# A vision transformer tower on one core: tokenizer and both attentions in an order written by hand, with a causal sum over tokens

## The chip, the core and the metric

The kernel runs on one core of a Trainium2 chip. The metric is the device time of one execution in microseconds (us). TensorE (PE in the profile) multiplies matrices and turns tiles, VectorE (DVE), ScalarE (ACT) and GpSimd (POOL) do the elementwise work, and SyncE (SP) issues most transfers. [...]

## What is computed

Thirty-two images of 256 x 256 x 3 are cut into 256 patches of 768 values and projected to 256 features. Two layers follow, each with an attention and a feed-forward part on layer-normalised features. Everything is float32.

```python
h = patches @ W.T + b                                   # tokenizer
# layer 0, gating attention:  xn = rms-normalised layernorm(h)
uv = silu(xn @ W_uv + b_uv); u, v, base = split(uv)
q, k = base * gamma[0] + beta[0], base * gamma[1] + beta[1]
h = h + (u * (relu(q @ k.T / sqrt(128)) ** 2 @ v)) @ W_o + b_o
# layer 0, feed-forward on the 127 best-ranked of 256 tokens (x = layernorm(h))
w = x @ wr + br;  y = (gelu(x[sel] @ w1 + b1) @ w2 + b2) * w[sel]
h = h + x + scatter(y)
# layer 1, phase attention (x = layernorm(h))
key, query = (tanh(gelu(x @ W1 + b1) @ W2 + b2) * freq * pi for both)
retrieved = causal sum over tokens of cos(query - key) * (x @ Wv + bv), / sqrt(positions * 64)
h = h + x + (layernorm(retrieved) * ln_w + ln_b) @ Wo + bo
# layer 1, attention experts: 4 heads x 4 experts, causal softmax, gates;
# the residual of head n is the projection of image n by head n, for all images
resid = sx[arange(4), arange(4)]
```

## The kernel before

All features H stay in on-chip memory, as one tile of 128 partitions x 2 x 256 per image. `bank()` (ppool) gives one of eight accumulator banks of 512 columns. `mm` (L114) is every matrix product, in float32, and appears in the profile as two passes of PE per product. `transposed` (L187) turns features with eight PE passes per pair of images; `copy_split` evicts the first half on ACT (L192) and the second on DVE (L194). `normed` (L173) makes layer-normalised features on DVE, `stats` (L122, L123) the mean and variance of a chunk, and `pow_rstd` (L147, L148) the inverse root on POOL.

There are five stages:

- **Tokenizer** (`unit_a`): one image per step, 24 passes of 256 columns, patches loaded by SP six images ahead.
- **Gating attention** (`unit_b`): one pair of images per unit, in five sections that `phase` staggers. The first normalises (L173), turns, and makes base, q and k (L394, L396). The second makes scores, gates (`uT`) and values (`bv`). The third makes the gated product (`gT`, L439), the output product, H (L452) and its statistics. The fourth is `norm_c` with the token weights (L341), the fifth `ranks`: `rank_c` turns the weights of an image into a bank (L349), DVE counts how many tokens are ahead (L354, L356), and POOL scatters the tokens to DRAM by rank (L365).
- **Feed-forward** (`step_c`): quads of images through w1 and w2; DRAM transfers gather the results. From step 8 on each step also takes one section of `prepare`, which folds the weights for layer 1.
- **Phase attention** (`turn`, `hidden`, `phases`, `values_d`, `match`, `memory`, `turn_back`, `output`): pairs of images, three steps apart. `memory` multiplies the causal match of keys and queries (`dat`) with the values (`dv`); the result is turned back and multiplied with wo1 in `output`. At step 21 `residuals` normalises, turns and projects images 0 to 3.
- **Experts** (`prep`, `scores`, `weights`, `values`, `post`): images six steps apart, in an order written out by hand.

Who sets the order differs by stage. Inside `tc.manual_schedule(engines=...)` each named engine gets its instructions in the order of the program text; elsewhere a planner orders them by its own costs. Before the change the tokenizer is written by hand for PE, ACT and SP only, the feed-forward and experts' loops for all five queues, and both attentions are left to the planner. The phase attention's program text is steered by

```python
ORDER = ((1, turn), (7, output), (4, match), (2, hidden), (5, memory), (3, phases), (6, turn_back),
         (3, values_d), (0, norm))
```

Of the kernel before, what the change touches and what calls it, by code (L numbers as in the profile page):

```python
# [31 lines left out]
F32 = mybir.dt.float32  # L33
# [6 lines left out]
P = 128  # L40
# [38 lines left out]
def vit_tower(tc, a, out):  # L79
# [116 lines left out]
    def one_step(active):  # L196
        return [g for g in active if next(g, g) is not g]

    def phase(unit, images, steps):

        active = []
        for b in range(0, B, images):
            active = one_step([unit(b)] + active)
        for _ in range(steps - 1):
            active = one_step(active)
        return active


# [35 lines left out]
    patches = a["patches"].rearrange("(k p) t -> p k t", p=P)  # L247
    with (
        tc.tile_pool(name="a_w", bufs=1) as pw,
        tc.tile_pool(name="a_x", bufs=6) as pp,  # L250
        tc.manual_schedule(engines={ENG.PE, ENG.Activation, ENG.SP}),
# [35 lines left out]
        loaded = []  # L287
        st_b = new_stats("b")

        def unit_a(b):  # L290
# [20 lines left out]
            if b == 4:  # L311
                loaded.extend(layer_0_weights())
            if b % 2:
                factors_b(b - 1)
            yield

        def factors_b(b):


            st, rs, i = at(st_b, b)  # L320
            q = slice(i * NC, (i + 2) * NC)
            var = st.rearrange("p i c s -> p (i c) s")[:, q, 1]
            low = spool.tile([P, 2 * NC], F32, name="low")
            pow_rstd(low, var)
            nc.gpsimd.tensor_scalar(rs[:, q], var, 1e-36, 1.0, ALU.max, ALU.mult)
            nc.gpsimd.tensor_tensor(rs[:, q], rs[:, q], minus_half[:, 0 : 2 * NC], ALU.pow)
            nc.vector.scalar_tensor_tensor(rs[:, q], low, 1e5, rs[:, q], ALU.mult, ALU.min)
            nc.vector.tensor_scalar(rs[:, q], rs[:, q], col("attn_g"), None, ALU.mult)

        phase(unit_a, 1, 2)  # L330
        wuv, row_b, wo, row_c, before, w1 = loaded

    def norm_c(b):
        x = px.tile([P, NC, D], F32, name="cx", bufs=6)
# [34 lines left out]
    with (  # L369
# [4 lines left out]
        scale = 1.0 / math.sqrt(128.0)  # L374

        def unit_b(b0):
            xs = []
            for j in range(2):
                x = p4.tile([P, NC, D], F32, name="bx")
                normed(x, b0 + j, st_b)  # L380
                xs.append(x)
                nc.gpsimd.tensor_tensor(
                    H[b0 + j], H[b0 + j], over(row_b("b_o"), [P, NC, D], 1), ALU.add
                )
            xT = p2.tile([P, 2, 2 * N], F32, name="bxT")
            transposed(xT, xs, copy_split)

            base = p2.tile([P, 2 * N], F32, name="base")
            p = bank()
            for k in range(2):  # L390
                mm(p, wuv[:, k, 1024:1152], xT[:, k, :], k == 0, k == 1)
            nc.scalar.activation(base, p, AF.Silu, bias=col("b_base"))
            q = p2.tile([P, 2 * N], F32, name="bq")
            nc.vector.tensor_scalar(q, base, col("gamma", 0), col("beta", 0), ALU.mult, ALU.add)  # L394
            kk = p2.tile([P, 2 * N], F32, name="bk")
            nc.vector.tensor_scalar(kk, base, col("gamma", 1), col("beta", 1), ALU.mult, ALU.add)  # L396

            yield
            attn = []
            for j in range(2):  # L400
                p = bank()
                for m in range(NC):
                    mm(p[:, m * N : (m + 1) * N], kk[:, j * N + m * P : j * N + (m + 1) * P], q[:, j * N : (j + 1) * N])
# [4 lines left out]
                attn.append(t)  # L408

            uT = p2.tile([P, 4, 2 * N], F32, name="uT")  # L410
            for hc in range(4):
                p = bank()
                for k in range(2):
                    mm(p, wuv[:, k, hc * P : (hc + 1) * P], xT[:, k, :], k == 0, k == 1)
                nc.scalar.activation(uT[:, hc, :], p, AF.Silu, bias=col("b_u", hc))
            vs = []
            for tb in range(2 * NC):
                p = bank()
                for k in range(2):
                    mm(p, xT[:, k, tb * P : (tb + 1) * P], wuv[:, k, 512:1024], k == 0, k == 1)  # L420
# [3 lines left out]
                vs.append(v)  # L424

            yield
            gTs = []
            for j in range(2):
                gT = p2.tile([P, 4, N], F32, name="gT")
                for half in range(2):  # L430
                    p = bank()
                    for h in range(2):
                        hc = 2 * half + h
                        for m in range(NC):
                            mm(
                                p[:, h * N : (h + 1) * N], vs[j * NC + m][:, hc * P : (hc + 1) * P],
                                attn[j][:, m, :], m == 0, m == NC - 1,
# [3 lines left out]
                        uT[:, 2 * half : 2 * half + 2, j * N : (j + 1) * N], ALU.mult,  # L441
                    )
                gTs.append(gT)
            if b0 == B - 2:
                turn_c(0, quads[0], 0)
            for j in range(2):
                b, gT = b0 + j, gTs[j]
# [8 lines left out]

            pow_rstd_of(st_c, b0, 2)

            yield
            normed_c[b0] = [norm_c(b0 + j) for j in range(2)]  # L460

            yield
            ranks(b0)
            if b0 in (2, 6):
                first_ranks(b0 - 2, quads[b0 // 4], 0)
# [9 lines left out]
        phase(unit_b, 2, 3)  # L475
# [26 lines left out]
    wv, wo1 = load(pwd, "wv1", nc.sync), load(pwd, "wo1", nc.sync)  # L502
# [3 lines left out]
    add_row = pwd.tile([P, D], F32, name="add_row")  # L506
    row_e = load_rows(pwe, "rows_e", ROWS_E, N_ROWS_E, nc.sync)
# [46 lines left out]
    def prepare():  # L554


        for w, g in ((wv, 2), (row_d("bv").unsqueeze(1), 1)):
# [3 lines left out]
            nc.vector.tensor_tensor(w, w, over(m, [P, g, D], 2), ALU.subtract)  # L561
        nc.gpsimd.memset(ones_row, 0.0)
# [10 lines left out]
        for k in range(2):  # L573
            mm(p[:, 0:D], col("ln_b", k).to_broadcast([P, P]), wo1[:, k, :], k == 0, k == 1)
        pa, pv = bank(), bank()
# [7 lines left out]
        nc.vector.tensor_tensor(add_row, p[:, 0:D], row_d("bo"), ALU.add)  # L583
# [49 lines left out]
        yield  # L633
        for k in range(2):
            nc.vector.tensor_scalar(wo1[:, k, :], wo1[:, k, :], col("ln_w", k), None, ALU.mult)
# [23 lines left out]
    def residuals(pool):  # L659
        for n in range(NH):  # L660
            xT = features(pool, normed_e(pool, n))
            p = bank()
            for c in range(NC):
                for k in range(2):
                    mm(
                        p[:, c * HD : (c + 1) * HD], xT[:, k, c * P : (c + 1) * P], hl[:, k, n * HD : (n + 1) * HD],
                        k == 0, k == 1,
                    )
            nc.vector.tensor_tensor(
                res[:, :, n, :], p[:, 0 : NC * HD].rearrange("p (c d) -> p c d", c=NC),  # L670
                over(row_e("hl_b")[:, n * HD : (n + 1) * HD], [P, NC, HD], 1), ALU.add,
            )
        centred(res8, res8, NC * NH)

# [4 lines left out]
    def norm_d(b0, s, pool, name, bufs):  # L679
        s.xs = []  # L680
        for j in range(2):
            x = pool.tile([P, NC, D], F32, name=name, bufs=bufs)
            normed(x, b0 + j, st_d)
            s.xs.append(x)
            h = H[b0 + j]
            nc.gpsimd.tensor_tensor(h, h, x, ALU.add)
            nc.gpsimd.tensor_tensor(h, h, over(add_row, [P, NC, D], 1), ALU.add)

    with region_c:
# [20 lines left out]
        def fetch(b0, s, half):  # L710
            s.y = s.y if half else []
            for b in range(b0 + 2 * half, b0 + 2 * half + 2):
                y = px.tile([P, NC, D], F32, name="cx", bufs=6)
# [889 lines left out]
```

## Time and profile before

| what | before |
|---|---|
| median of 3 runs (lowest, highest) | 2049.75 us (2048.95, 2054.02) |
| the profiled execution | 2053.58 us, span 2051.8 us |
| PE busy | 1973.4 us (96%) |
| DVE / ACT / POOL busy | 1334.2 / 832.5 / 731.1 us |
| mean granted PE clock | 0.977 |
| tokenizer, first to last product | 9 to 173 us of the span |
| gating attention | 173 to 712 us |
| feed-forward | 712 to 956 us |
| phase attention | 956 to 1333 us |
| experts and the end | 1333 to 2052 us |

The span is the time on the profiler's clock from the first to the last instruction; the execution's own time is 1.8 us longer. A share is busy time over the span. The stage borders are read from the timeline at the last product of a stage. The chain of waits that ended last lies to 90% on PE.

### The profile page before, as it was taken

The page shows a single profiled execution, that of the slowest core. Times are in us where ns is not written, and L with a number is a line of the kernel's source. Part 1 is how long each engine was busy: PE and PEld are TensorE (multiplying, and loading weights), DVE is VectorE, ACT ScalarE, POOL GpSimd, SP SyncE. Part 2 cuts the span into 40 slices and gives each one's busy share as a digit, 9 for nine tenths or more (in the row PEclk, how much of TensorE's full clock was granted, in tenths as well). Part 3 has the DMA queues.
Part 4 walks back from the last instruction along what each step waited for, and adds up shares of the span by engine and source line. Part 5 has one row for each costly group of instructions (what it writes and reads, how often), then busy time and mean ns, then how long its engine had stood idle before and what let it go on. Part 6 is the DMA issues. An engine that isn't in the chain of part 4 may idle for free.

```text
span 2051.8 us, 38271 instructions
## 1 busy us (share of the span) xinstructions
PE 1973.4 (96%) x15412; PEld 1431.7 (70%) x15412; DVE 1334.2 (65%) x3591; ACT 832.5 (41%) x1569; POOL 731.1 (36%) x691
## 2 busy tenths in 40 slices
PE   9998999999999899999999999999999999999983
PEld 8885676666667657666667677667777777777762
DVE  2335557667675634435655566547898989998986
ACT  0001322222221121222443444367777777777762
POOL 1224224334341443336432333103444444444443
PEclk9999999999999999999998999989999999999996
DMA  9540000000000222221000000001121212121212
GB/s 296 151 135 1 0 1 31 18 24 16 16 18 29 87 81 72 60 70 57 1 0 1 1 1 1 1 17 38 39 63 43 64 43 63 44 62 45 64 48 53
DMA packets 69687, 95.12 MB, mean 46 GB/s; under 512 B 8576, under 2 KB 50944, under 8 KB 69120
## 3 DMA queue, kind: packets, MB, share of 16 engines
q1 hardware_dynamic: 62784, 75.04, 13.1%
q0 software_dynamic: 6144, 16.79, 2.7%
q8 instruction: 123, 2.02, 0.4%
q10 hardware_dynamic: 576, 0.79, 0.1%
q14 instruction: 60, 0.49, 0.1%
HBM read 46.45 MB, written 20.97 MB: 33 GB/s over the span
## 4 chain that ended last, share of the span: by engine, by line
PE 90%; DVE 5%; DMA 1%; ACT 1%; issue 1%; POOL 1%; SPq 0%; DVEq 0%; ACTq 0%; POOLq 0%
PE bank L114 85%; PE bank L646 2%; PE bank L187 2%; PE bank L1148 1%; DMA both<-hx 1%; PE bank L349 1%; DVE bank L994 0%; ACT bxT L192 0%; DVE fout L1157 0%; PE bank L240 0%; DMA patch<-in_patches_dram 0%; DMA cx<-results,rank_of 0%; DVE six L122 0%; DVE two L1079 0%; DVE fout L1153 0%
## 5 line engine op out<-in xcount | busy, mean ns | idle before, releaser
L996 ACT ACTIVATE et<-bank 128x512 f32<-128x512 f32 x384 | 202.4, 598 | 59.0 <-DVE bank L994 58.3
L114 PEld LDWEIGHTS bank<-ev,et 128*64 128x64 f32 x6144 | 198.0, 137 | 33.8 <-ACT et L996 21.3
L994 DVE TENSOR_TENSOR bank<-bank,w_tri 128x256 f32<-128x256 f32 (+1 forms) x384 | 173.6, 514 | 69.6 <-PE bank L114 67.6
L114 PE MATMUL bank<-ev,et 128*64 128x74 f32 (+1 forms) x6144 | 210.9, 226 | 0.0
L1074 POOL TENSOR_TENSOR eo<-eo,gate 128x1024 f32<-128x1024 f32 x64 | 121.9, 1925 | 226.5 <-DVE gate L1071 207.9
L114 PE MATMUL bank<-g,sx 64*128 64x512 f32 (+1 forms) x512 | 192.7, 506 | 0.7 <-ACT g L954 0.7
L114 PE MATMUL bank<-g,sw 64*128 64x512 f32 (+1 forms) x512 | 191.8, 506 | 0.0
L114 PE MATMUL bank<-tokW,patch 128*128 128x256 f32 x768 | 166.7, 380 | 2.3 <-DMA patch<-in_patches_dram 2.3
L114 PEld LDWEIGHTS bank<-tokW,patch 128*128 128x128 f32 x768 | 146.1, 190 | 23.0 <-issue 2.7
L114 PE MATMUL bank<-bxT,w_wuv 128*128 128x512 f32 x320 | 149.2, 605 | 5.5 <-ACT bxT L192 3.9
L192 ACT COPY bxT<-bank 128x512 f32<-128x512 f32 x16 | 9.4, 586 | 342.6 <-PE bank L187 342.6
L1026 POOL TENSOR_TENSOR hv<-hv,minus_half 128x8 f32<-128x8 f32 x64 | 119.5, 1867 | 5.3
L1012 ACT COPY eo<-bank 128x286 f32<-128x286 f32 x256 | 97.2, 421 | 58.3 <-PE bank L114 51.8
L114 PE MATMUL bank<-xsel,w_w 128*128 128x512 f32 x256 | 113.3, 600 | 0.0
L114 PE MATMUL bank<-attn,bv 128*128 128x256 f32 x512 | 113.3, 379 | 0.0
L114 PE MATMUL bank<-w_wo,gT 128*128 128x256 f32 x512 | 113.1, 379 | 0.0
L114 PE MATMUL bank<-w_w,hT 128*128 128x256 f32 x512 | 113.1, 379 | 0.0
L114 PE MATMUL bank<-w_wuv,bxT 128*128 128x512 f32 x256 | 112.5, 592 | 0.0
L114 PEld LDWEIGHTS bank<-attn,bv 128*128 128x128 f32 x512 | 97.1, 190 | 19.5 <-issue 6.9
L114 PEld LDWEIGHTS bank<-w_w,hT 128*128 128x128 f32 x512 | 96.7, 190 | 15.8 <-issue 3.3
L114 PEld LDWEIGHTS bank<-w_wo,gT 128*128 128x128 f32 x512 | 97.2, 190 | 13.2
L114 PEld LDWEIGHTS bank<-bxT,w_wuv 128*128 128x128 f32 x320 | 59.8, 192 | 66.3 <-issue 53.0
(245 smaller groups left out, 3980.2 us busy)
## 6 DMA issues: line engine op xcount, KB each, us to landing
patch<-in_patches_dram SPq DMA_DIRECT2D x31, 768.0 KB, 4.7
sw<-sx SPq DMA_DIRECT2D x64, 128.0 KB, 2.4
both<-fxT SPq DMA_DIRECT2D x64, 128.0 KB, 2.5
both<-hx SPq DMA_DIRECT2D x64, 128.0 KB, 2.3
out_dram<-fout SPq DMA_DIRECT2D x32, 256.0 KB, 2.5
cs<-ranked SPq DMA_DIRECT2D x32, 128.0 KB, 3.0
results<-cy SPq DMA_DIRECT2D x32, 128.0 KB, 1.7
w_w<-in_w_dram SPq DMA_DIRECT2D x2, 1024.0 KB, 10.2
```

The costliest lines, as they stand in the source:

```text
L114: nc.tensor.matmul(o, lhsT, rhs, start=first, stop=last)
L187: nc.tensor.transpose(p[:, o : o + P], x[:, c, k * P : (k + 1) * P], ident)
L192: nc.scalar.copy(o, i)
L349: nc.tensor.transpose(pw[:, c * P : (c + 1) * P], w[:, c : c + 1].to_broadcast([P, P]), ident)
L646: nc.tensor.transpose(p[:, o : o + P], x[:, c, k * P : (k + 1) * P], ident)
L994: nc.vector.tensor_tensor(own, own, over(tri, [P, n_e, P], 1), ALU.add)
L996: nc.scalar.activation(t, p, AF.Exp)
L1012: nc.scalar.copy(im.o[:, c * NH + n, 0:OC], p[:, 0:OC])
L1026: nc.gpsimd.tensor_tensor(v, v, minus_half, ALU.pow)
L1074: nc.gpsimd.tensor_tensor(im.mix[k], im.mix[k], over(im.gate[:, :, 2 * k : 2 * k + 2], [P, NC * NH, 2, HD], 3), ALU.mult)
L1148: nc.tensor.transpose(im.po[:, o : o + P], im.fT[:, k, c * P : (c + 1) * P], ident)
```

## The change

All five queues are put under the written order from the start of the tokenizer to the end of the phase attention (`by_hand`). The generator-based `unit_b` becomes separate functions (`norm_b`, `turn_b`, `base_b`, `queries_b`, `scores_b`, `gates_b`, `values_b`, `gated_b`, `output_b`) in one loop. The first two pairs are normalised after images 26 and 28 of the tokenizer, and the first pair is turned and multiplied to base, q and k before the last image. In each later step the ranks stand between base and queries, and the next pair is normalised at the end.

```diff
+    by_hand = ExitStack()
+    by_hand.enter_context(tc.manual_schedule(engines={ENG.PE, ENG.DVE, ENG.Activation, ENG.Pool, ENG.SP}))
...
+    def norm_b(b0, s):
+        s.xs = []
+        for j in range(2):
+            x = px.tile([P, NC, D], F32, name="cx", bufs=8)
+            normed(x, b0 + j, st_b)
+            s.xs.append(x)
+            h = H[b0 + j]
+            nc.gpsimd.tensor_tensor(h, h, over(row_b("b_o"), [P, NC, D], 1), ALU.add)
...
+        for b in range(B):
+            if b == B - 1:
+                half = [p0.tile([P, 4, D], F32, name="cs", bufs=2).rearrange("p j d -> p (j d)") for _ in range(2)]
+                turn_b(0, pairs_b[0], p0, "xsel")
+                base_b(0, pairs_b[0], half[0][:, 0 : 2 * N])
+                queries_b(0, pairs_b[0], half[0][:, 2 * N :], half[1][:, 0 : 2 * N])
+            unit_a(b)
+            if b == 4:
+                wuv, row_b, wo, row_c, before, w1 = layer_0_weights()
+            if b % 2:
+                powers = powers_b(b - 1)
+            elif b:
+                factors_b(*powers)
+            if b in (B - 6, B - 4):
+                u = (b - B + 6) // 2
+                norm_b(2 * u, pairs_b[u])
...
+        for t in range(B // 2 + 2):
+            def pair(u):
+                return (2 * u, pairs_b[u]) if 0 <= u < B // 2 else None
+
+            new, old, older = pair(t) if t else None, pair(t - 1), pair(t - 2)
+            if new:
+                turn_b(*new, p2, "bxT")
+                base_b(*new, p2.tile([P, 2 * N], F32, name="base"))
+            if t >= 4:
+                ranks(2 * (t - 4))
+                if t in (5, 7):
+                    first_ranks(2 * t - 10, quads[t // 2 - 2], 0)
+            if new:
+                queries_b(*new, p2.tile([P, 2 * N], F32, name="bq"), p2.tile([P, 2 * N], F32, name="bk"))
+            if old:
+                scores_b(*old)
+                gates_b(*old)
+                values_b(*old)
+            if t == 1:
+                factors_b(*powers)
+            if t >= 3:
+                normed_c[2 * (t - 3)] = [norm_c(2 * (t - 3) + j) for j in range(2)]
+            if older:
+                gated_b(*older)
+                if t == B // 2 + 1:
+                    turn_c(0, quads[0], 0)
+                output_b(*older)
+            if 2 <= t + 1 < B // 2:
+                norm_b(*pair(t + 1))
```

In the phase attention the causal sum runs over the tokens' features themselves, and Wv and Wo are applied afterwards in one product of 512 columns: `wvo` holds wv beside wv times wo1, `memory` multiplies the features xs with `dat`, and `output` multiplies the sum with wvo. The first 256 columns give the statistics of the retrieved values, the other 256 are added to H by `add_output` one step later. `values_d` and `turn_back` are gone. The biases go into the features and weights: `norm_d` makes features plus one, and `prepare` subtracts what the one adds (`bias_d`, `add_row`, and bv spread over wv).

```diff
+        q = bank()
+        for k in range(2):
+            mm(q[:, 0:D], ones_d, wv[:, k, :], k == 0, k == 1)
+        for i, w in enumerate((wk1, wq1)):
+            for m in range(2):
+                o = D + 2 * i + m
+                for k in range(2):
+                    mm(q[:, o : o + 1], w[:, k, m * P : (m + 1) * P], ones_d[:, 0:1], k == 0, k == 1)
...
+                nc.tensor.transpose(p[:, o : o + P], wv[:, k, m * P : (m + 1) * P], ident)
...
+                mm(p[:, k * D : (k + 1) * D], wvT[:, m, k * P : (k + 1) * P], wo1[:, m, :], m == 0, m == 1)
+        nc.vector.tensor_copy(wvo[:, :, D:], p.rearrange("p (k d) -> p k d", k=2))
...
+                t, x, p = s.t[j], s.xs[j], bank()
+                for k in range(2):
+                    o, d = k * N, slice(k * P, (k + 1) * P)
+                    mm(p[:, o : o + N], x[:, 0, d], t[:, 0:N], True, False)
+                    mm(p[:, o + P : o + N], x[:, 1, d], t[:, N : N + P], False, True)
+                m = p8.tile([P, 2, N], F32, name="dm", bufs=4)
+                nc.scalar.copy(m.rearrange("p k n -> p (k n)"), p)
...
+        def output(b0, s):
+            st_m = spool.tile([P, 2 * NC, 2], F32, name="d_st")
+            s.po = []
+            for q in range(2 * NC):
+                m, c, p = s.m[q // NC], q % NC, bank()
+                for k in range(2):
+                    mm(p, m[:, k, c * P : (c + 1) * P], wvo[:, k, :], k == 0, k == 1)
+                six = spool.tile([P, 6], F32, name="six")
+                nc.vector.bn_stats(six, p[:, 0:D])
+                nc.vector.bn_aggr(st_m[:, q, :], six)
+                s.po.append(p)
...
+            do(1, turn)
+            do(7, add_output)
+            if t != 4:
+                do(4, match)
+            do(7, stats_e)
+            do(1, residual_d)
+            do(2, hidden, 0)
+            if t == 5:
+                match(0, pairs[0])
+            do(2, hidden, 1)
+            do(5, memory)
+            do(3, phases)
+            if t:
+                do(0, norm_d, p8, "dx", 4)
+            do(6, output)
+            if 3 <= t <= 5:
+                step_c(END_C + t - 3)
```

`residuals` is gone as well: in the experts' stage `prep` projects the turned features of each of the images 0 to 3, which it has anyway, with head b's weights and stores them in `res`.

```diff
+                if b < NH:
+                    p = bank()
+                    for c in range(NC):
+                        for k in range(2):
+                            mm(
+                                p[:, c * HD : (c + 1) * HD], im.xT[:, k, c * P : (c + 1) * P],
+                                hl[:, k, b * HD : (b + 1) * HD], k == 0, k == 1,
+                            )
...
+                if b == NH - 1:
+                    centred(res8, res8, NC * NH)
```

## The prediction

> **What bounds the kernel now.** I read the page's engine totals and slices first, then the busy time by stretch, cut at the stage borders, then the timeline at those borders and inside one period of each stage. TensorE (PE) is busy for 1973.4 of 2051.8 us, and the chain of waits puts 90% on it, so a cost or a gain counts only where it makes PE work longer or stand still. The stretches (columns: length, then PE, PEld, DVE, ACT, POOL busy and instruction count, granted clock, DMA share, GB/s):
>
> ```profile
> 173.00:205.60 32.60, 26.77 (x72) 12.98 (x72) 20.30 (x35) 10.14 (x16) 15.66 (x14) 0.84 0.00 1
> 205.60:667.00 461.40, 457.88 (x1670) 303.46 (x1671) 294.12 (x721) 108.50 (x170) 158.58 (x148) 1.00 0.05 17
> 667.00:721.00 54.00, 45.12 (x183) 32.64 (x183) 37.96 (x126) 7.77 (x12) 22.63 (x25) 0.94 0.28 89
> 978.00:1101.00 123.00, 122.97 (x596) 84.63 (x598) 74.00 (x187) 51.87 (x72) 44.38 (x46) 0.99 0.00 1
> 1101.00:1121.00 20.00, 16.09 (x88) 13.89 (x85) 8.34 (x21) 6.47 (x10) 1.20 (x2) 0.74 0.00 1
> ```
>
> The reader should see that the gating attention (205.6 to 667) and the phase attention (978 to 1101) leave PE almost no gap, while the three borders (tokenizer to gating, gating to feed-forward, the residuals at 1101) do. So the written order has little to win inside the first attention and can only lose there; its gains lie at the borders and in PE work that vanishes.
>
> One period of the gating attention, from the timeline (start, length, engine, line):
>
> ```profile
> 513.83 2.00 DVE L173 TENSOR_SCALAR bx<-h,st_b,rs_b 128x256 f32<-128x256 f32 x3
> ...
> 525.97 7.07 PE L114 MATMUL bank<-w_wo,gT 128*128 128x256 f32 x32
> ...
> 533.07 0.69 DVE L452 TENSOR_TENSOR h<-h,bank 128x512 f32<-128x512 f32 x1 [1.76 <-PE bank L114]
> 533.09 1.04 PE L187 MATMUL bank<-ident,bx 128*128 128x128 f32 x8
> ```
>
> The normalised features bx (L173) were made 19 us before PE turns them (L187). PE starts the turn at 533.09 right behind the output product, while DVE only begins to add that product (L452). The period is 33.06 us (T at 500.04 to 533.09). PE's own work in it: 16 passes of 512 columns each for gates and values at 0.43 us (13.8), 32 of 256 each for gated and output at 0.2155 (13.8), scores 8 x 0.2155 (1.7), base 4 x 0.43 (1.7), 12 turns at 0.12 (1.45): 32.5. Only 0.55 us waits.
>
> How two image ranks follow each other when the order is written, in the feed-forward stage:
>
> ```profile
> 729.89 0.38 PE L349 MATMUL bank<-ident,cw 128*128 128x128 f32 x2
> 732.43 0.43 PE L349 MATMUL bank<-ident,cw 128*128 128x128 f32 x2 [2.15 <-DVE ctmp L356]
> ```
>
> Both images of a pair use one bank, pw: PE cannot turn the second until DVE has read the first (four L354/L356 operations, 730.31 to 732.37). In the first attention the planner puts other matmuls between the two.
>
> The phase attention's PE period, 21.85 us:
>
> ```profile
> 1231.95 3.62 PE L114 MATMUL bank<-w_wo,drT 128*128 128x256 f32 x16
> ...
> 1240.54 3.60 PE L114 MATMUL bank<-dxT,w_wq 128*128 128x512 f32 x8
> 1243.97 2.75 PE L114 MATMUL bank<-dv,dat 128*128 128x256 f32 x12
> ...
> 1248.54 1.10 PE L187 MATMUL bank<-ident,dr 128*128 128x128 f32 x8
> 1249.47 3.62 PE L114 MATMUL bank<-w_wv,dxT 128*128 128x256 f32 x16
> ```
>
> [...] so a turn that waits holds all PE work behind it. The trace agrees: at 732.43 PE stood with the next 16 matmuls' operands ready. [...] after 4.91 us idle at 978.03 the 16 dz passes took 2.93 us against 1.58 at 1235.50; after the 2.15 us at 732.43 the next 16 were at full rate (7.03). [...] Here one L173 takes 0.40 us alone and three take 2.00 beside L382.
>
> **The change part by part** (against the profiled span of 2051.8; that execution took 2053.58, 3.8 above the median of 2049.75, to which I add the difference).
>
> First pair ahead of the last image: 173.0 to 205.65 holds 32.65 us for PE work of 24 turns (2.9), two bases (3.4), scores, gates, values (15.5): 21.8, so 10.85 are lost. Afterwards two short waits for copies, about 1.3: **-9.5** (bounds -8 and -10.5).
>
> Gating attention, wait 1: norm_b(t+1) is now DVE's last work of step t, behind output_b, and the turn is PE's first work of step t+1. After PE's last output pass DVE does L452 (0.7 with the signal), two statistics (1.05), four L173 (0.33 each alone, 0.67 beside POOL: 1.3 to 2.7, I take 1.65); three turns fit under the last of them (-0.35). PE stands **3.05** us (2.6 to 3.6), where today it stands none. Everything of step t+1 queues behind it. 13 steps: 39.7, and 2.4 for the first, which has no output: 42.
>
> Wait 2: ranks in mid-step. PE turns image one, then waits for DVE, then image two; scores, whose operands are ready, queue behind. 2.2 us (2.0 to 2.6) by the row above; 12 steps, and two last ones where DVE first ends the output's tail (4.0): 34.
>
> Wait 3: norm_c stands on DVE ahead of the gT products: 5.9 us (4 L173, 4 L341 of which two meet POOL's L336 at 1.48, two L344), begun 0.85 after the values end; the first gT is ready at 7.45, while gated ends at 6.9: output_b starts 0.7 late (0.3 to 1.2), 15 steps: 10.5. Of today's waits 3 go. POOL's four indirect DMAs (2.9 us apart) now stand ahead of the attn squares, which the next step needs: about 18 us of slack, nothing. A gap near 3 us may meet the slow clock: a quarter of the steps at up to 1.7 us, and 2 more: 7 (0 to 25). Sum of this stage: **+91** (67 to 129).
>
> Border to feed-forward: today hidden_c's second half ends 27.7 us after the last output pass, behind ranks at 2.90 and 4.46 us of idle. Written, the ranks of pair 14 wait 4, hidden 6.9, ranks of pair 15 wait for their norm_c, hidden 6.9: about 23: **-4.7**.
>
> prepare: 2 x 256 columns (0.9), 16 one-column passes [...](2.1), four turns (0.5), four products of 256 (1.7); PE has no gap there: **+5.1**. SP moves the same weight bytes, and w2 still goes first when the attention's memory is free: 10.2 us of landing against about 20 until its first use, nothing.
>
> Phase attention: values (3.45), turn_back (0.93), output (3.55) go: -7.93; output with 512 columns is 16 x 0.43 = 6.88; memory 8 x 0.2155 + 8 x about 0.12 = 2.7, as before. Net 1.05 per pair: **-16.8**. norm_d is 5.7 us behind the phases (tanh 0.85, four z operations 2.8, norm 2.0) and lies under output's 6.9. The four output banks stay until add_output; with eight banks hidden may wait 0 to 0.65: I take 0.3, **+4.5**. The start loses its values as cover: PE waits about 5.8 for the second pair's norm where it waited 4.9: **+1.5**.
>
> Residuals: they stand behind the values product of 1102.66, and the next dz product starts at 1126.25, where a normal period (7.88 from values to dz) gives 1110.5: 15.7 lost. They leave this stage. In the experts' stage 4 x 8 passes of about 0.12 return, and a little DVE: 5. **-10.7**. The end of the stage: add_output, statistics and the first norm run after each other: 6.6 us until the first turn, where today 2.4: **+5** with the shorter pipeline drained.
>
> Sum: -9.5 + 91 - 4.7 + 5.1 - 16.8 + 4.5 + 1.5 - 10.7 + 5 = **+65**, so 2049.75 + 65 = 2115.
>
> **Rivals.** (1) Faster: norm_b does not end up as the late one, and PE finds its operands ready; then only wait 3 is left of the stage: -26 + 7, some 2031. One mechanism: the order of DVE's queue around output_b. Everything outside the stage sums to -26, so it decides at 26/14 = 1.9 us of wait per step. For it: norm_b depends on nothing of output_b. Against: in the stages already written by hand, DVE's rows follow the text. (2) Only one of waits 1 and 2 is real (for example, the second image's turn finds its bank read): 91 - 34 or - 42: 2073 to 2081. (3) The clock drops after each gap: 13 to 14 steps at 1.7 more: 2135 to 2145. (4) The shorter sum over tokens does not shorten PE, as 512 columns cost twice 256: that is in the sum, and why it brings 17 and not 60.
>
> **How the numbers follow.** Waits 1 and 2 both: 0.64; rival 2: 0.12; rival 3: 0.10; rival 1: 0.14. About 0.3% (6 us) is what a measurement of this kernel tells from no change; 0.02 of rival 1 and 0.02 of rival 2, with their bounds, lie within it. Faster 0.12, same 0.04, slower 0.64 + 0.10 + 0.10 = 0.84. The likeliest case alone spans 2080 to 2150; down to rival 2: 2062 to 2150.
>
> **What would show it.** In the profile after: L187 turns behind DVE's normalisation with about 3 us of idle per gating step; L349 with about 2.2 us; period 38 to 39 us instead of 33.06; phase attention 20.8 to 21.4; no gap at 173, none at 1101. A gating period under 35 us would make it wrong.

## The result and the profile after

The kernel after takes 2131.17 us (median of 4 runs, 2128.69 to 2136.35) against 2049.35 us before (4 runs, one more than in the table above): ratio 1.0401, 95% interval 1.0373 to 1.0429. It is slower by 81.8 us; the prediction had 2115 and a range of 2062 to 2150. The profiled execution took 2131.89 us, its span is 2130.1 us (2051.8 before: +78.3), its mean granted clock 0.965 (the share of its full clock that PE was granted; 0.977 before).

The busy-time part of the page after shows PE busy for 28 us more than before, although the causal sum of tokens has less for it to do:

```profile
PE 2001.6 (94%) x15108; PEld 1401.7 (66%) x15108; DVE 1299.4 (61%) x3605; ACT 823.6 (39%) x1549; POOL 726.3 (34%) x692
```

The busy time by stretch of the kernel after (length, PE, PEld, DVE, ACT, POOL with instruction counts, granted clock, DMA share, GB/s) says where. The rows are the border from tokenizer to gating attention, the gating attention, its last three steps, and the middle of the phase attention:

```profile
177.30:205.00 27.70, 24.39 (x75) 12.55 (x74) 10.41 (x21) 9.78 (x16) 7.54 (x9) 1.00 0.00 1
205.00:724.00 519.00, 464.99 (x1532) 300.55 (x1530) 261.49 (x686) 98.47 (x153) 151.29 (x143) 0.92 0.04 14
724.00:819.60 95.60, 85.98 (x305) 60.26 (x306) 51.88 (x148) 16.06 (x24) 30.60 (x30) 0.91 0.08 28
1106.00:1379.00 273.00, 273.00 (x1145) 153.43 (x1144) 154.92 (x456) 116.48 (x157) 96.33 (x104) 1.00 0.00 1
```

In the gating attention, where PE had been busy for 457.88 of 461.40 us at clock 1.00, it now stands still for 54 of 519 us, and its mean granted clock is 0.92. The middle of the phase attention has no gap at all. Cut at the last product of each stage, as in the prediction:

| up to | before, us | after, us | stage longer by | predicted |
|---|---|---|---|---|
| end of gating attention | 711.9 | 819.6 | +107.7 | +81.5 |
| end of feed-forward | 956.7 | 1063.9 | -0.4 | +0.4 |
| end of phase attention | 1332.7 | 1414.8 | -25.1 | -26.5 |
| end of span | 2051.8 | 2130.1 | -3.9 | +10 |

(The predicted column puts the 15.7 us of the residuals in the phase attention and their 5 us, with the 5 of the stage's end, in the experts.)

One period of the gating attention, from the timeline of the kernel after (start, length, engine, line, and in brackets idle time before, with its releaser):

```profile
509.02 2.48 DVE L451 TENSOR_TENSOR gT<-bank,uT 128x512 f32<-128x512 f32 x4
509.81 7.12 PE L115 MATMUL bank<-w_wo,gT 128*128 128x256 f32 x32
...
516.97 0.69 DVE L464 TENSOR_TENSOR h<-h,bank 128x512 f32<-128x512 f32 x1 [1.56 <-PE bank L115]
...
518.78 1.37 DVE L174 TENSOR_SCALAR cx<-h,st_b,rs_b 128x256 f32<-128x256 f32 x4
...
519.24 2.30 PE L188 MATMUL bank<-ident,cx 128*128 128x128 f32 x8 [2.30 <-DVE cx L174]
...
521.36 2.79 PE L115 MATMUL bank<-bxT,w_wuv 128*128 128x512 f32 x4
...
526.52 0.69 PE L380 MATMUL bank<-ident,cw 128*128 128x128 f32 x2 [2.15 <-DVE ctmp L387]
...
527.00 3.30 PE L115 MATMUL bank<-bq,bk 128*128 128x256 f32 x8
```

The reader is to see four things. First, the output product ends at 516.93, and only then does DVE add it, take its statistics and normalise the next pair (518.78); PE's turns wait 2.30 us for the first normalised half and then crawl behind the others (2.30 us for eight instead of 1.04). Second, the second image's ranks wait 2.15 us for DVE. Third, after each gap the products cost more: 2.79 us for the four of base (1.98 where nothing stalled), 3.30 for the eight of scores (1.89). Fourth, the output product starts at 509.81, when the gated product is done, and finds the first gT there: wait 3 of the prediction is missing. The period is 560.20 - 519.24 = 40.96 us.

One period of the phase attention from the same timeline:

```profile
1105.99 1.58 PE L115 MATMUL bank<-dz 64*128 64x256 f32 x16
...
1114.47 2.78 PE L115 MATMUL bank<-dat,dx 128*128 128x256 f32 x16
...
1119.06 7.13 PE L115 MATMUL bank<-wvo,dm 128*128 128x512 f32 x16
1126.03 1.04 PE L188 MATMUL bank<-ident,dx 128*128 128x128 f32 x8
1127.00 1.58 PE L115 MATMUL bank<-dz 64*128 64x256 f32 x16
```

The values product and the turn back are gone, the output product has 512 columns and takes 7.13 us; the period is 21.01 us (1105.99 to 1127.00) where it was 21.85.

### The profile page after: what moved, and what is told of

It is laid out like the page before. It is cut to its first block, busy times and chain, and to the rows that moved or that the text cites. A ratio compares the mean times of both kernels' runs of the same rounds, so it can differ in the third digit from the quotient of the medians.

```text
span 2130.1 us, 37646 instructions
## 1 busy us (share of the span) xinstructions
PE 2001.6 (94%) x15108; PEld 1401.7 (66%) x15108; DVE 1299.4 (61%) x3605; ACT 823.6 (39%) x1549; POOL 726.3 (34%) x692
## 3 DMA queue, kind: packets, MB, share of 16 engines
q1 hardware_dynamic: 62912, 75.04, 12.4%
q8 instruction: 121, 1.98, 0.4%
## 4 chain that ended last, share of the span: by engine, by line
PE 92%; DVE 6%; DMA 1%; ACT 1%; issue 0%; SPq 0%; POOL 0%; ACTq 0%; DVEq 0%
PE bank L115 86%; PE bank L719 2%; PE bank L188 2%; DVE ctmp L387 1%; DVE ctmp L385 1%; PE bank L1222 1%; DVE six L123 1%; PE bank L380 1%; DVE h L464 1%; DMA both<-hx 0%; DMA patch<-in_patches_dram 0%; DVE cx L174 0%; PE bank L229 0%; DVE fout L1231 0%; DVE two L1153 0%
## 5 line engine op out<-in xcount | busy, mean ns | idle before, releaser
L434 DVE TENSOR_TENSOR bv<-bank,rows_b 128x512 f32<-128x512 f32 x64 | 44.3, 692 | 186.6 <-PE bank L115 186.6
L115 PE MATMUL bank<-wvo,dm 128*128 128x512 f32 x256 | 114.1, 599 | 0.0
L123 DVE BATCH_NORM_STATS2 six<-h 128x6 f32<-128x256 f32 x256 | 105.6, 413 | 4.4
```

Source lines behind the costliest of these rows:

```text
L115: nc.tensor.matmul(o, lhsT, rhs, start=first, stop=last)
L123: nc.vector.bn_stats(six, x)
L434: nc.vector.tensor_tensor(v, p, row_b("b_v"), ALU.add)
```

## The experiments

All kernels start from the text after; each edit is shown against it. "After" has two new gaps in a gating step: norm_b late (wait 1) and the two images' ranks one behind the other (wait 2). The first five experiments take them away one at a time or together, or fill one or both with work.

**Next pair normalised early.** In the text, norm_b of the next pair moves from behind output_b to right behind queries_b.

```diff
                 queries_b(*new, p2.tile([P, 2 * N], F32, name="bq"), p2.tile([P, 2 * N], F32, name="bk"))
+            if 2 <= t + 1 < B // 2:
+                norm_b(*pair(t + 1))
...
                 output_b(*older)
-            if 2 <= t + 1 < B // 2:
-                norm_b(*pair(t + 1))
```

> The changed kernel with one move: the next pair is normalised right after the queries of the step, 20 us earlier on DVE, not after output_b. Theory (two waits, each with its price, plus a slow clock after the longer one): the idle 2.4 us ahead of the turns goes and with it the half-rate turns and base; the wait of 2.15 us between the two images' rank turns stays, at full clock. Period of the first attention 35 to 35.5 us (40.96 in the changed kernel, 33.06 before), 13 periods, time 2053 to 2062. Rival A (the norm is not what is late, another queue of the written order is): period and time unchanged, 2131. Rival B (the rank wait alone trips the clock too): period 36.8 to 37.5, time 2075 to 2085.

Measured: 2080.49 us (2079.67 to 2082.21), ratio to before 1.0156 (1.0134 to 1.0179), 50.7 us less than after; period 37.50. The timeline of this kernel:

```profile
485.16 1.04 PE L188 MATMUL bank<-ident,cx 128*128 128x128 f32 x8
...
491.38 0.54 PE L380 MATMUL bank<-ident,cw 128*128 128x128 f32 x2 [2.15 <-DVE ctmp L387]
491.71 3.51 PE L115 MATMUL bank<-bq,bk 128*128 128x256 f32 x8
```

The turns start right behind the output product and take 1.04 us. Only base's short waits for its copies (0.24 and 0.32 us) are left in the step beside the gap of 2.15 us at the ranks, and the scores behind that gap are still at half rate (3.51 us against 1.89). The theory had put them at full clock; rival B came true, in period and time: the slow clock does not need both gaps.

**Ranks turned together.** The weights of both images are turned into the bank before DVE reads it.

```diff
             pw = bank()
             for j in range(2):
+                w = normed_c[b0][j][1]
+                for c in range(NC):
+                    o = j * N + c * P
+                    nc.tensor.transpose(pw[:, o : o + P], w[:, c : c + 1].to_broadcast([P, P]), ident)
+            for j in range(2):
                 rank_c(b0 + j, *normed_c[b0][j], pw[:, j * N : (j + 1) * N])
...
     def rank_c(b, x, w, pw):
-        for c in range(NC):
-            nc.tensor.transpose(pw[:, c * P : (c + 1) * P], w[:, c : c + 1].to_broadcast([P, P]), ident)
```

> The changed kernel with one move: the weights of both images of a pair are turned into the bank before DVE reads it, so PE does not wait between them. Theory with the slow clock put down to the norm's gap alone: 2.4 us go per step, about 3.4 us of half rate stay; period 38 to 38.8 us, some 8 us more at the three ranks without a turn ahead of them; time 2090 to 2098. Rival (the clock drops only because both gaps fall into one stretch): the half rate goes as well; period 35.2 to 35.8, time 2045 to 2055. Rival (the bank is not shared in a way that counts): unchanged, 2131.

Measured: 2077.03 us (2075.28 to 2079.14), ratio 1.0134 (1.011 to 1.0158), 54.1 less than after; period 37.55. The theory and both rivals missed. In the timeline the other gap is left with its own half-rate products:

```profile
498.86 1.74 PE L188 MATMUL bank<-ident,cx 128*128 128x128 f32 x8 [2.30 <-DVE cx L174]
500.83 3.52 PE L115 MATMUL bank<-bxT,w_wuv 128*128 128x512 f32 x4 [0.24 <-ACT bxT L193]
```

My theory had kept the slow scores when the rank gap goes; they went with it. The rival had the clock recover altogether; it did not. Each gap has its own drop: base pays for wait 1 (3.52 us here against 1.98), scores for wait 2 (3.51 us in the run before, 1.89 here).

**Both moves together.**

```diff
+                    nc.tensor.transpose(pw[:, o : o + P], w[:, c : c + 1].to_broadcast([P, P]), ident)
...
                 queries_b(*new, p2.tile([P, 2 * N], F32, name="bq"), p2.tile([P, 2 * N], F32, name="bk"))
+            if 2 <= t + 1 < B // 2:
+                norm_b(*pair(t + 1))
```

> Both moves together. Theory: nothing of the two waits is left, the first attention runs at its PE work: period 32.6 to 33.1 us; with the gains of the other stages the kernel is then faster than before the change: 2012 to 2026. Rival (the written order of this stage costs something else, such as the gT products behind norm_c or POOL's scatters): period 34 us or more, 2035 to 2060.

Measured: 2020.07 us (2018.15 to 2020.26), ratio 0.9859 (0.9837 to 0.9881), 111.1 less than after: the two single gains add up to 104.8. The time is the theory's; the period is 0.35 over its 33.1, as base waits 0.24 and 0.32 us for its copies. The timeline shows a step without either gap, 33.44 us long, and the mean granted clock from 177 to 711 us is 1.00:

```profile
462.87 1.04 PE L188 MATMUL bank<-ident,cx 128*128 128x128 f32 x8
...
466.99 1.89 PE L115 MATMUL bank<-bq,bk 128*128 128x256 f32 x8
...
496.31 1.04 PE L188 MATMUL bank<-ident,cx 128*128 128x128 f32 x8
```

So the whole loss of the change sits in two places of the text of one loop, and the rest of the change is a gain of 1.4%.

**One gap filled.** Five products of zeros into a free bank behind norm_b, so that PE works during wait 1. This adds work and leaves nothing out.

```diff
             if 2 <= t + 1 < B // 2:
                 norm_b(*pair(t + 1))
+                p = bank()
+                for _ in range(5):
+                    mm(p[:, 0:N], zero[:, 0:P], zero)
```

> The changed kernel, with five products of a zero tile into a bank that nobody reads after each step's output_b, 2.2 us of PE work into the gap ahead of the turns; it adds work and leaves out none. Theory (the slow clock after the gap costs about 3.4 us a step): the turns, base and scores run at full rate, period 37.3 to 37.9 us, time 2084 to 2095, faster than the changed kernel with less work. Rival (the turns are slow because their operands or evictions come late, not because of the clock): period 41 us or a little more, 2131 to 2136.

Measured: 2108.15 us (2107.45 to 2109.42), ratio 1.0291 (1.0268 to 1.0313). With 10 more passes per step the kernel is 23 us faster than after: base behind the filled gap takes 1.98 us where it took 2.79, and the mean granted clock of the profiled run is 0.978 against 0.965. The gain is smaller than the theory's (13 us over its upper end): steps of 38.38 and of 40.07 us mostly take turns, as the scores behind wait 2, whose 2.15 us are in every step, run at full rate (1.89 us) in one step and slower (2.5 to 3.4) in the next.

**Both gaps filled.** The same five products also ahead of the second image's turn, in steps with a new pair.

```diff
     def rank_c(b, x, w, pw, fill=False):
+        if fill and b % 2:
+            p = bank()
+            for _ in range(5):
+                mm(p[:, 0:N], zero[:, 0:P], zero)
...
-                ranks(2 * (t - 4))
+                ranks(2 * (t - 4), t < B // 2)
```

> The changed kernel with zero products in both gaps of a step: five after output_b as in the run before, and five between the two images' rank turns; nothing is left out, both waits of the written order stay. Theory (both waits and a slow clock after either): no step runs at half rate, every period is the 38.4 us of those steps of the run with one gap filled in which the scores were at full rate; that is 33.45 + 4.95 of waits, and the clock's share of the changed kernel's 40.96 is 2.6. Time 2097 to 2103. Rival (the half rate after the rank gap comes from somewhere else, such as the relu or bank evictions): period stays at 38.4 and 40.1 in turn, 2108.

Measured: 2098.45 us (2096.16 to 2100.2), ratio 1.023 (1.0209 to 1.0251). In the timeline the zero products stand where the gaps were, and every period with ranks in it is 38.4 us, as the theory had it; base takes 1.98 us and the scores 1.89 in all of them:

```profile
460.81 2.32 PE L115 MATMUL bank<-zero 128*128 128x256 f32 x10
...
467.28 2.32 PE L115 MATMUL bank<-zero 128*128 128x256 f32 x10
...
499.19 2.32 PE L115 MATMUL bank<-zero 128*128 128x256 f32 x10
```

This splits a step of after: 40.96 = 33.45 (both moves) + 4.94 of waiting (38.39 here less 33.45) + 2.57 of slow clock (40.96 less 38.39).

The next two undo one part of the change each, on top of both moves, so that the gating steps are out of the way. They were measured apart from "both moves", so the ratios to before are compared.

**Residuals as a function of their own again,** at step 21 of the phase attention.

```diff
+            if t == 21:
+                residuals(p2)
...
-                if b < NH:
-                    p = bank()
...
-                if b == NH - 1:
-                    centred(res8, res8, NC * NH)
```

> The kernel with both waits repaired (2020.1), and the residuals computed again by a function of their own at step 21 of the phase attention, not from the experts' own features. Theory (the residuals cost 15.7 us where they stood, and 5 where they stand now): slower by 8 to 13 us, 2028 to 2033. Rival (the 15.7 were the planner's placing, or the experts' stage gives the work for nothing): within 4 us, or slower by 15 or more.

Measured: 2036.13 us (2034.2 to 2039.07), ratio 0.9933 (0.9917 to 0.9949), 0.0074 or 15 us over both moves; with the two intervals that is some 10 to 21 us, which does not tell the theory's 13 from the rival's 15. The traces do. In the timeline of this kernel PE goes from image to image, waiting for one DVE operation and one copy each time:

```profile
1089.86 7.13 PE L115 MATMUL bank<-wvo,dm 128*128 128x512 f32 x16
1098.53 0.87 PE L721 MATMUL bank<-ident,ex 128*128 128x128 f32 x4 [1.54 <-DVE ex L174]
1100.08 1.97 PE L115 MATMUL bank<-w_hl,exT 128*128 128x64 f32 x8 [0.68 <-ACT exT L731]
1102.84 1.14 PE L721 MATMUL bank<-ident,ex 128*128 128x128 f32 x4 [0.79 <-DVE ex L174]
...
1117.52 2.87 PE L115 MATMUL bank<-dz 64*128 64x256 f32 x16
```

From the output product to dz lie 27.66 us, against 7.94 with both moves (984.00 to 991.94). That is 19.7 more, and 1.3 in the slow dz products; less the 3.3 that the projection costs in the experts' stage (below), 17.7, and the two spans differ by 18.0 (2034.1 and 2016.1). So the rival's number came true, but not its reason, that the experts' stage gives the work for nothing. The gaps are short (0.7 to 1.5 us), yet the mean clock in 1090 to 1125 is 0.71 and the dz products behind take 2.87 us instead of 1.58.

**First two pairs normalised, and the first turned, only behind the last image.** (`half = ...` stands for the lines that turn the first pair and make its base, q and k.)

```diff
             if b == B - 1:
-                half = ...          # turn_b, base_b, queries_b of pair 0
             unit_a(b)
...
-            if b in (B - 6, B - 4):
-                u = (b - B + 6) // 2
-                norm_b(2 * u, pairs_b[u])
+            if b == B - 1:
+                for u in range(2):
+                    norm_b(2 * u, pairs_b[u])
+                half = ...          # turn_b, base_b, queries_b of pair 0
```

> The kernel with both waits repaired, and the first two pairs normalised, turned and multiplied after the last image of the tokenizer. Theory (the start of the first attention was worth 9.5 us of waits, by the border before): slower by 7 to 11 us, 2027 to 2031. Rival (in a written order the border closes without that, since the second pair's turns cover the first one's copies): slower by under 4 us.

Measured: 2025.86 us (2024.34 to 2026.06), ratio 0.9878 (0.9858 to 0.9898). That is 0.0019 over both moves with intervals that overlap; in the traces, the third pair's turns, the first ones of the regular loop, come 5.9 us later (201.89 against 195.97). The ratios give 3.9 us, at the edge of the rival; the traces lie between the two expectations. The timeline:

```profile
176.43 1.65 PE L188 MATMUL bank<-ident,cx 128*128 128x128 f32 x8 [2.38 <-POOL low L148]
178.32 3.57 PE L115 MATMUL bank<-xsel,w_wuv 128*128 128x512 f32 x4 [0.24 <-ACT xsel L193]
```

So moving the first pair ahead is worth about 6 us at this border in a written order, by the traces; once more the first products after the gap are at half rate (3.57 for four, against 1.98).

**The gating loop left to the planner.** The text after, but the written order is closed ahead of the gating loop and opened again behind it.

```diff
+    by_hand.close()
     with (
         tc.tile_pool(name="b_2", bufs=2, reuse_waits="tile") as p2,
...
     region_b.close()
+    by_hand.enter_context(tc.manual_schedule(engines={ENG.PE, ENG.DVE, ENG.Activation, ENG.Pool, ENG.SP}))
```

> The changed kernel with its program text as it is, but the loop of the first attention left to the planner again; tokenizer, feed-forward and phase attention keep the written order. Theory (the loss is the order of the queues, not the text's operations): the planner sets norm_b and the rank turns where it had them, period 33.1 to 33.6 us, 2015 to 2030, near the kernel with both waits repaired. Rival (the planner follows the text and keeps the norm behind output_b, or the text needs the wait, by a buffer): period 37 us or more, 2080 or more.

Measured: 2032.65 us (2031.49 to 2033.97), ratio 0.992 (0.9899 to 0.994), 2.7 us over the upper end of the theory and far from the rival. The timeline:

```profile
503.04 1.04 PE L188 MATMUL bank<-ident,cx 128*128 128x128 f32 x8
...
510.14 0.43 PE L380 MATMUL bank<-ident,cw 128*128 128x128 f32 x2 [1.03 <-DVE ctmp L387]
510.40 6.17 PE L115 MATMUL bank<-bxT,w_wuv 128*128 128x512 f32 x14
...
537.10 1.04 PE L188 MATMUL bank<-ident,cx 128*128 128x128 f32 x8
```

The planner puts base, scores and gates between the two images' turns; 1.03 us of wait 2 is left, nothing of wait 1, no slow clock (14 products of 512 columns in 6.17 us), and the period is 34.06 us. The same functions in the planner's order are not slow: the written order is.

**Two more reorderings.** On top of both moves, scores stand between turn and base (PE has work while the turned features are copied), and the phase attention normalises its second pair at step 1. A second kernel also turns that pair ahead of the first pair's phases.

```diff
                 turn_b(*new, p2, "bxT")
+            if old:
+                scores_b(*old)
+            if new:
                 base_b(*new, ...)
...
             if old:
-                scores_b(*old)
...
-            if t:
+            if t == 1:
+                norm_d(2, pairs[1], p8, "dx", 4)
+            elif t > 3:
                 do(0, norm_d, p8, "dx", 4)
```

> The kernel with both waits repaired and two more moves: the scores of the pair before stand between turn_b and base_b, as cover for the copies (0.57 us of waits in each of 15 steps), and the second pair of the phase attention is normalised at its step 1, not behind the first pair's phases (4.57 and 2.50 us idle, and a slow clock after them). Theory: period 32.9 us, the gap at the phase attention's start under 2 us: faster by 12 to 17 us, 2003 to 2008, below both kernels. Rival (the copies or the norm are late for another reason, DVE's queue): faster by under 6 us.

```diff
-            do(1, turn)
+            if t != 4:
+                do(1, turn)
...
+            if t == 3:
+                turn(2, pairs[1])
             do(3, phases)
```

> The best kernel so far (2000.4), with the turns of the phase attention's second pair put ahead of the first pair's phases, so that ACT copies them before it takes up tanh and sine (where it stood 7.04 us behind the sine). Theory (the early norm won nothing since the wait went over to ACT's queue): the gap falls from 7.04 to about 2.5 us ahead of match, and the slow clock after it mostly goes: faster by 4 to 7 us, 1993 to 1997. Rival (the wait goes on to the next, gelu behind the sine, or match): within 2 us.

Measured: 2000.4 us (2000.13 to 2004.19), ratio 0.9761 (0.9744 to 0.9779), and 1994.89 us (1993.4 to 1997.61), ratio 0.9736 (0.9718 to 0.9755). The second is the fastest version of this study, 2.6% under before, and in its expected range; the first is 2.6 us faster than expected, though one of its two moves failed. The timeline of the first, at a gating step and at the start of the phase attention:

```profile
484.91 1.04 PE L188 MATMUL bank<-ident,cx 128*128 128x128 f32 x8
485.78 1.89 PE L115 MATMUL bank<-bq,bk 128*128 128x256 f32 x8
487.51 1.88 PE L115 MATMUL bank<-bxT,w_wuv 128*128 128x512 f32 x4
...
951.30 6.15 PE L115 MATMUL bank<-dxT,w_wk 128*128 128x512 f32 x8 [7.04 <-ACT dxT L193]
```

The gating period is 32.36 us, 1.1 less than with both moves, and base no longer waits. The start of the phase attention, where the gap was to fall under 2 us, gained nearly nothing: the wait that had been DVE's normalisation became one for ACT's copy, which stood in ACT's queue behind the first pair's phases. Turning the pair ahead of the phases cuts it, as the timeline of the second kernel shows:

```profile
950.93 1.68 PE L115 MATMUL bank<-dz 64*128 64x256 f32 x16 [3.38 <-ACT dz L876]
```

7.04 us of idle became 3.38 (about 2.5 was expected), now for the phases themselves.

## Why the prediction was right, and where it was not

The direction and its cause were right: 2131 lies in the range, and the two waits are in the profile at the lines that the prediction named. Several sizes were off, and they ran against each other: the clock cost 25 us more than its term, wait 3 cost 10.5 less, and the experts and the end came out 14 less. That 2131 lies only 16 us from 2115 is in part luck.

**Waits 1 and 2: right.** Predicted 3.05 us of standing and 2.2. Measured: 2.30 of idle plus 0.69 in turns that follow L174 (1.73 for eight when only that slows them, against 1.04), so 3.0; and 2.15. Together a step loses 4.94 by the filled kernel, because a smaller wait of base (0.32 us for DVE's copy) goes. The last ranks waited 3.71 us each, predicted 4.0. The likeliest case asked for a period of 38 to 39 us; with the clock out of the way it is 38.39, while the kernel after itself, at 40.96, lies above it.

**Clock: the step that failed.** The term was 7 us, for a quarter of the steps; that share was my estimate, and no trace of before showed it. Measured: 2.57 us in every settled step; over the 13 periods from 198.18 to 724.04 after takes 525.86 us, the filled kernel 493.78, so 32 us, above the upper bound of 25. Rival 3, the clock that drops after each gap, fits the traces (base 2.79 us behind the first gap, scores 3.30 behind the second); its 1.7 us per step were too few as well, and its total of 2135 to 2145 lies above the measured one only because other terms were too high. The premise was wrong: one gap of 2.15 us with full-rate products behind it (732.43 of before, 7.03 us for sixteen) was read as typical. A gap of this length can go either way, as the first two steps with ranks show in the kernel with the next pair normalised early:

```profile
268.16 0.43 PE L380 MATMUL bank<-ident,cw 128*128 128x128 f32 x2 [2.15 <-DVE ctmp L387]
268.43 1.89 PE L115 MATMUL bank<-bq,bk 128*128 128x256 f32 x8
...
303.97 0.69 PE L380 MATMUL bank<-ident,cw 128*128 128x128 f32 x2 [2.15 <-DVE ctmp L387]
304.45 3.28 PE L115 MATMUL bank<-bq,bk 128*128 128x256 f32 x8
```

The same gap is followed by scores at full rate in the first and at little more than half in the second, and in every step from there on they take 3.3 us or more. In the kernel after, the first step with ranks already has 2.95 us (at 279.98), the later ones 3.3 to 3.5.

**Wait 3: 10.5 predicted, none measured.** The order of DVE's queue was read rightly; the size was off. The timeline ahead of the period shown:

```profile
502.90 7.07 PE L115 MATMUL bank<-attn,bv 128*128 128x256 f32 x32
...
503.71 0.73 DVE L174 TENSOR_SCALAR cx<-h,st_c,rs_c 128x256 f32<-128x256 f32 x2
```

norm_c starts 0.81 us behind the end of the values (502.90), where the prediction had 0.85, and stands ahead of the gT products. But it takes 5.31 us (503.71 to 509.02) and not 5.9, so the first gT is ready at 509.71, 6.81 and not 7.45 behind the values, and the gated product ends at 509.81. A tenth of a us keeps this wait away. With both moves it is the same: the output product starts at 489.36 with no wait before it.

**The account of the gating attention.** Before has 13 turns' periods in 427.94 us (204.32 to 632.26), after 525.86: +97.9, of which both moves keep 6.2 (434.13), waiting is 59.6 (493.78 - 434.13), and the clock 32.1. The start of these periods came 6.1 earlier (198.18), and the last three steps took 15.9 longer (95.6 against 79.6). The sum is 107.7.

**First pair ahead: right as a reading, with a smaller cause.** What the border costs PE, idle time and slow clock together, fell from 10.85 us (5.8 of them idle, by the first row of the prediction) to 1.51 (waits of 0.24, 0.66, 0.24 and 0.37 at full clock), so 9.3 where 9.5 was predicted. But the experiment that keeps the written order and takes away the early pair loses 6, not 9.5: the rest comes with the written order itself.

**Phase attention: right.** Predicted -1.05 per pair for the products and +0.3 for the banks, together -0.75; measured 21.01 - 21.85 = -0.84. There is no wait for a bank at output or hidden. At the start PE idles for 4.57 and 2.50 us where it idled for 1.38 and 4.91: 0.8 more, against +1.5. Slow products follow in both: the eight hidden ones take 5.07 us instead of 3.70, where before the sixteen of dz took 2.93 instead of 1.58.

**Residuals: right in kind, too small.** In the experts' stage the projection costs 3.3 us (first to sixth turn 79.74 us, 76.45 with the function back), predicted 5. With the 15.7 read from the trace of before, the move is worth 12.4, predicted 10.7. In the written order the function in its old place would cost more, a net 15 by the ratios and 18 by the profiles.

**End of the phase attention: the sign was wrong.** I had add_output, statistics and the first norm one after the other, +5. The timeline of before and, below it, that of after at the first experts' turn:

```profile
1335.24 0.84 PE L646 MATMUL bank<-ident,ex 128*128 128x128 f32 x4 [2.44 <-DVE st_e L123]
1336.80 3.78 PE L114 MATMUL bank<-exT,w_hl 128*128 128x256 f32 x8 [0.72 <-ACT exT L656]
```

```profile
1404.20 0.40 DVE L174 TENSOR_SCALAR ex<-h,st_e,rs_e 128x256 f32<-128x256 f32 x1
...
1407.94 7.03 PE L115 MATMUL bank<-wvo,dm 128*128 128x512 f32 x16
...
1414.81 0.60 PE L719 MATMUL bank<-ident,ex 128*128 128x128 f32 x4
...
1416.12 1.99 PE L115 MATMUL bank<-exT,w_hl 128*128 128x256 f32 x8 [0.72 <-ACT exT L729]
```

The first image belongs to the first pair, done long before; DVE normalises it at 1404.20, ahead of the last output's statistics, and PE turns it right behind the output product. The gap of 2.44 us is gone and with it the half rate behind it (3.78 against 1.99): the first two turns are 10.20 us apart instead of 15.23. With the 3.3 of the residuals the stage comes to about -4, as the table has it. I had taken the last pair's chain for that of the first image.

Rival 1 (norm_b not late) is out for the kernel as it stands, and its order was one of the two edits that made the kernel fast. Rival 2 (only one wait real) is out as well: both are in the trace, and either one alone costs 57 to 60 us over both moves.

**What stays open.** Not shown is why a loop with such a gap meets the slow clock in every step once settled, where the first step with ranks of the norm-early kernel did not (1.89 us). The turns of after are 41.76 us apart at 313.45, then 41.45, 41.27, 41.10, 40.99, 40.98, and 40.96 from there to the end; the kernels with one gap settle at 37.55 (ranks turned together) and 37.50 (norm early). The kernels without a drop stand at 33.45 (both moves), 38.39 (both gaps filled) and 34.06 (the planner's order), and with one gap filled, steps of 38.38 and of 40.07 mostly take turns. No run shows what fixes these periods, and none shifted a step by a part of a us to see whether the drop goes. Open is also whether the idle time alone counts. Around both waits PE does nothing but turns: from the output product to base 4.3 us pass (496.56 to 500.83 with the ranks turned together), from base to the scores 2.7 (489.00 to 491.71 with the norm early). No run kept the idle time and took the turns away.

## What to carry to other kernels

When an order is written by hand, ask of each section which engine does its last operation, and put the producer of the next step's first product ahead of the consumer of this step's last one; one passage in the wrong place cost over 50 us here, twice, while the rest of the change gained 29. Price a PE gap with its length and the half rate behind it: a gap of some 2 us in a loop cost nearly twice itself here (2.15 became 4.05 per step, 37.50 less 33.45). And a wait that was moved rather than shortened turned up in the next queue, as the copy on ACT did (7.04 us).

## What was not expected of the hardware

The clock dropped behind gaps of 2.15 and 2.30 us, each without the other in its step, in every step once the loop had settled (scores 3.51 us against 1.89, base 3.52 against 1.98); with the first gap filled, the second one still did it in about every other step (2.5 to 3.4 us against 1.89). In the residuals, with gaps of 0.7 to 1.5 us and short turns and products between them, the mean clock was 0.71 from 1090 to 1125. And the period of a loop with such a gap was not its work plus its gap: with the 2.15 us alone it was 37.50 us, where 33.45 and 2.15 make 35.60.
